# Attention softmax: mask, negation, move to SBUF and row minimum in one VectorE operation

## The chip, the cores and the metric

The kernel runs on one core of a Trainium2 chip. The metric is the device time of one execution, in microseconds (us), median over runs; the profile was taken from one execution on the same core. The engines are TensorE (PE, with its weight loads as PEld), VectorE (DVE), ScalarE (ACT), GpSimd (POOL) and SyncE (SP), which here only issues transfers.

## The reference

A batch of 8 images of 384 channels and 32x32 positions (1024 tokens) goes through two layers, all in float32. Layer 0 is a state-space block: RMS norm, input projection, a short convolution, a scan with 16 states over the tokens forwards and backwards, a gate, an output projection, and a depthwise 3x3 convolution beside it. Layer 1 is attention and a feed-forward network with sign-binarized weights and quantized activations. The change is in the attention:

```python
scores = jnp.einsum('bhqd,bhkd->bhqk', q, k)          # 6 heads of 64
causal = jnp.tril(jnp.ones((T, T), dtype=bool))        # T = 1024
scores = jnp.where(causal, scores, -jnp.inf)
attn = jax.nn.softmax(scores, axis=-1)
out = jnp.einsum('bhqk,bhkd->bhqd', attn, v)
```

The binarization of the two feed-forward weights subtracts the mean of each of five groups of output rows; the change touches how that mean is scaled.

## The kernel before, in words

**The scan** is cut into 768 units of two states by 512 tokens by 128 channels. For each unit POOL multiplies the input by the broadcast B row (`s_first`, L588), ACT makes the decays `da` in PSUM (L601), DVE runs two scans in place in `g` (L606), POOL multiplies by the broadcast C row (L612), and PE adds the unit into the PSUM tile `y` with eight transposing products (`s_sum`, L620). There are six `g` buffers, and POOL's first product for a unit runs two units ahead of the scan (`AHEAD = 2`), so a `g` buffer comes free for POOL when PE has read it at L620.

**The attention** of one image runs over three pairs of heads (`c`) and two halves of the queries (`g`). `probabilities` goes over four blocks of 128 queries (`i`) and, for each, one or two blocks of up to 512 keys (`kb`): 36 pairs of score tiles an image, 288 in all, two heads (`e`) to a pair. For each pair PE makes the scores of the two heads in two PSUM banks (tag `s`, two banks in all; L786), with 64 rows each, and in the blocks that hold the diagonal adds the causal mask by a product of a bf16 identity with a bf16 mask (L797). DVE takes the negated row maximum from PSUM (L808), ACT takes the exponential from PSUM with that as bias, writes it to the SBUF tile `pr` and sums the row (L809). `weighted_values` then transposes the probabilities on PE (L861), ACT copies them to SBUF (L863), PE multiplies them with the values (L874), and DVE scales the product by factors that undo the block maxima (L829 to L838, L888 to L891).

**Order.** The kernel writes its steps into lists with an estimated cost each. `spread_over` merges lists in proportion to their costs: the score steps of one (c, g) are merged with the weighted values of the one before. The scan units are merged with attention and feed-forward steps by due times, so that attention of one image runs beside the scan of the next ones; the attention of the last image of `ORDER` runs alone at the end. The framework's scheduler then fixes the order of each engine's in-order queue; `pin` and `at_once` keep the score products of the two heads next to each other. [...] one bank for `y`, two for `da`, two for `s`, two for `pt`, one for `av`. The SBUF tile `pr` comes from the pool `mid` of ten buffers.

Of the kernel before, what the change touches and what calls it, by code (L numbers as in the profile page):

```python
# [9 lines left out]
F32 = mybir.dt.float32  # L10
BF16 = mybir.dt.bfloat16
AF = mybir.ActivationFunctionType
ALU = mybir.AluOpType
AX = mybir.AxisListType
# [3 lines left out]
P = 128  # L18
B, C, H, W = 8, 384, 32, 32
L = H * W  # L20
NC = C // P
HB = 512
# [9 lines left out]
GROUPS = 5  # L32
# [5 lines left out]
MASKED = -1e30  # L38
# [16 lines left out]
def kernel(  # L55
# [16 lines left out]
    nc = tc.nc  # L72
    pin = tc.keep_in_program_order

    const = ctx.enter_context(tc.tile_pool(name="const", bufs=1))
    small = ctx.enter_context(tc.tile_pool(name="small", bufs=4))
# [7 lines left out]
    def ctile(name, shape, dt=F32):  # L84
        return const.tile(shape, dt, name=name, tag=name)

    def btile(name):
        return big.tile([P, NC, L], F32, name=name, tag="big")

    def mtile(name, n=L):  # L90
        return mid.tile([P, n], F32, name=name, tag="mid")
# [7 lines left out]
    def bank(name, tag=None):  # L99
        if tag is None:  # L100
            turn[0] += 1
            tag = ("s", "pt")[turn[0] % 2]
        return ps.tile([P, HB], F32, name=name, tag=tag, bufs=BANKS[tag])
# [4 lines left out]
    def chunk(c):  # L108
        return slice(c * P, (c + 1) * P)
# [29 lines left out]
    for d in range(2):  # L139
        nc.scalar.dma_start(out=wdt[d * DW : d * DW + RANK, :], in_=w_dt)  # L140
        nc.scalar.dma_start(
            out=wdt[d * DW + RANK : d * DW + RANK + 1, :],
# [12 lines left out]

    ident = ctile("ident", [P, P])
    make_identity(nc, ident)
    identb = ctile("identb", [P, P], BF16)
    nc.vector.tensor_copy(identb, ident)
    cmask = mtile("cmask", P)  # L160
    make_causal_mask(nc, cmask, mask_val=MASKED)
    cmaskb = ctile("cmaskb", [P, P], BF16)
    nc.vector.tensor_copy(cmaskb, cmask)
    onesc = ctile("onesc", [P, P])
    nc.gpsimd.memset(onesc, 1.0 / C)
    onecol = ctile("onecol", [P, 1])
# [29 lines left out]
    def binarize(src, dst, nk, nout, per, name, emit):  # L196

        gs = nout // GROUPS
        st = {}

        def part(w, k, n):
            return w[k * P : (k + n) * P, :].rearrange("(k p) e -> p k e", p=P)

        def view(k, n):
            t = btile(f"{name}_{k}")
            v = t.rearrange("p c l -> p (c l)")[:, : n * nout].rearrange("p (k e) -> p k e", k=n)
            nc.scalar.dma_start(out=v, in_=part(src, k, n))
            return v

        starts = list(range(0, nk, per))  # L210

        @emit
        def _():
            st["ones"] = small.tile([P, P], F32, name=f"ones_{name}", tag="bones", bufs=1)
            nc.vector.memset(st["ones"], 1.0 / (gs * nk * P))
            st["mps"] = bank(f"mps_{name}", "av")

        for k in starts:

            @emit  # L220
            def _(k=k, n=min(per, nk - k)):
                v = view(k, n)
                sums = small.tile([P, GROUPS], F32, name=f"sums_{name}_{k}", tag="bsums", bufs=1)
                for g in range(GROUPS):
                    nc.vector.tensor_reduce(
                        sums[:, g : g + 1], v[:, :, g * gs : (g + 1) * gs], AX.XY, ALU.add
                    )
                nc.tensor.matmul(
                    out=st["mps"][:, :GROUPS],
                    lhsT=st["ones"],  # L230
                    rhs=sums,
                    start=(k == 0),
                    stop=(k == starts[-1]),
                )

        @emit
        def _():
            st["mean"] = small.tile([P, GROUPS], F32, name=f"mean_{name}", tag="bmean", bufs=1)
            nc.vector.tensor_copy(st["mean"], st["mps"][:, :GROUPS])

        for k in starts:

            @emit
            def _(k=k, n=min(per, nk - k)):
                v = view(k, n)
                for g in range(GROUPS):
                    z = v[:, :, g * gs : (g + 1) * gs]
                    nc.vector.tensor_scalar(z, z, st["mean"][:, g : g + 1], None, ALU.subtract)
                t = btile(f"sg_{name}_{k}")
                sg = t.rearrange("p c l -> p (c l)")[:, : n * nout].rearrange("p (k e) -> p k e", k=n)  # L250
                z, sg = v[:, :, : GROUPS * gs], sg[:, :, : GROUPS * gs]
                nc.scalar.activation(sg, z, AF.Sign)
                nc.vector.tensor_tensor(sg, sg, z, ALU.subtract)
                nc.vector.tensor_tensor(z, z, sg, ALU.add)
                nc.vector.memset(v[:, :, GROUPS * gs :], 0.0)
                nc.scalar.dma_start(out=part(dst, k, n), in_=v)
# [417 lines left out]
    def attention(b, emit_ffn, emit):  # L674
        st = {}
# [82 lines left out]
        def at_once(second):  # L758
            return tc.high_priority(offset=HURRY) if second else nullcontext()

        def rows_of(e):
            return slice(e * HD, (e + 1) * HD)

        def blocks_of(n):
            return [(k0, min(k0 + HB, n)) for k0 in range(0, n, HB)]

        def probabilities(c, g, steps):


            nb = g + 1  # L770

            def scores(i, qi, n, kb, k0, k1):
                pr = mtile(f"pr_{b}_{c}_{qi}_{kb}").rearrange("p (e l) -> p e l", e=2)
                st["pr", c, g, i, kb] = pr
                if kb == 0 and i == 0:
                    for what in ("nm", "rs"):
                        st[what, c, g] = small.tile(
                            [P, QT, 2, nb], F32, name=f"{what}_{b}_{c}_{g}", tag=f"{what}{nb}"
                        )
                nm, rs = st["nm", c, g], st["rs", c, g]  # L780
                ss = [bank(f"s_{b}_{c}_{qi}_{kb}_{e}", "s") for e in range(2)]

                order = (1, 0)
                for e in order:
                    with at_once(e == order[1]):
                        mm = nc.tensor.matmul(  # L786
                            out=ss[e][:, : k1 - k0],
                            lhsT=st["q"][rows_of(e), c, chunk(qi)],
                            rhs=st["k"][rows_of(e), c, k0:k1],
                            start=True,  # L790
                            stop=(k1 < n),
                        )
                    if e == order[1]:
                        pin(mm)
                if k1 == n:
                    for e in order:
                        mm = nc.tensor.matmul(  # L797
                            out=ss[e][:, k1 - k0 - P : k1 - k0],
                            lhsT=identb,
                            rhs=cmaskb,  # L800
                            start=False,
                            stop=True,
                        )
                        pin(mm)
                for e in range(2):
                    s = ss[e][:, : k1 - k0]
                    m = nm[:, i, e, kb : kb + 1]
                    nc.vector.tensor_reduce(m, s, AX.X, ALU.max, negate=True)  # L808
                    nc.scalar.activation(  # L809
                        pr[:, e, : k1 - k0], s, AF.Exp, bias=m, accum_out=rs[:, i, e, kb : kb + 1]  # L810
                    )

            for i in range(QT):
                qi = g * QT + i
                n = (qi + 1) * P
                for kb, (k0, k1) in enumerate(blocks_of(n)):
                    steps(lambda i=i, qi=qi, n=n, kb=kb, k0=k0, k1=k1: scores(i, qi, n, kb, k0, k1))
# [404 lines left out]
```

## Time and profile before

| | |
|---|---|
| time, median of 3 runs | 5189.24 us (5177.72 to 5191.12) |
| span of the profiled execution | 5182.2 us, 51037 instructions |
| PE busy | 4203.1 us, 81% |
| PE weight loads busy | 2254.6 us, 44% |
| POOL busy | 3688.1 us, 71% |
| DVE busy | 3562.3 us, 69% |
| ACT busy | 2701.1 us, 52% |
| mean granted TensorE clock | 0.876 of full speed |

A row of the groups gives the line and engine, the operation, what is written from what, the shape, the count, and then the busy time in us with the mean of one in ns, and the idle time of the engine just before these instructions with what ended most of it. A row of waits gives who waited for whom: us in total, times, and the longest. A row of the windows gives the busy time of each engine in one stretch and the number of its instructions. "issue" is time in which the profile shows nothing that was waited for. The busy time of PE is modelled, since its matmuls overlap.

### The profile page before, as it was taken

The numbers are of one execution on the slowest core, as the hardware profiler recorded it, in microseconds if no ns is written. First come the engines' busy times: TensorE is split into PE (matmuls) and PEld (weight loads), VectorE is DVE, ScalarE is ACT, GpSimd is POOL, SyncE is SP. The second block draws the span as 40 slices with busy tenths as digits, with TensorE's granted clock in tenths as the row PEclk, the third lists the DMA queues.
The fourth block names the chain that finished last, engine by engine and source line by source line (L and its number), as shares of the span: only waits on it lengthen the run. The fifth ranks groups of instructions, "written<-read, shape, count | busy, mean of one in ns | idle before, by whom it ended". The sixth has DMA issues, their size and how long they took to land. (4 is left out here: it accounts for less than half of the span.)

```text
span 5182.2 us, 51037 instructions
## 1 busy us (share of the span) xinstructions
PE 4203.1 (81%) x16842; PEld 2254.6 (44%) x16842; DVE 3562.3 (69%) x4206; ACT 2701.1 (52%) x4891; POOL 3688.1 (71%) x1944
## 2 busy tenths in 40 slices
PE   3687787888878788888887888878889888888798
PEld 1243443444434444444543444434445444444444
DVE  6887887667886667876687856778666665565522
ACT  4565564555645556545556445564454454453334
POOL 0578687877679776787777788677878977787600
PEclk7788797889889899898998888988988889989888
DMA  6554545324463234543343533336333234224200
GB/s 228 197 184 152 200 167 190 111 80 156 152 216 114 88 103 146 198 143 112 109 153 121 201 126 103 118 125 221 122 103 126 88 106 166 87 70 150 82 33 25
DMA packets 365009, 696.38 MB, mean 134 GB/s; under 512 B 30104, under 2 KB 88904, under 8 KB 364744
## 3 DMA queue, kind: packets, MB, share of 16 engines
q1 hardware_dynamic: 355232, 676.97, 38.8%
q10 hardware_dynamic: 9512, 16.15, 0.9%
q8 instruction: 133, 2.18, 0.2%
q14 instruction: 132, 1.08, 0.1%
HBM read 527.33 MB, written 165.68 MB: 134 GB/s over the span
## 5 line engine op out<-in xcount | busy, mean ns | idle before, releaser
L588 POOL TENSOR_TENSOR g<-ud,bc 128x1024 f32<-128x1024 f32 x768 | 1836.3, 2391 | 737.0 <-PE y L620 586.5
L612 POOL TENSOR_TENSOR g<-g,bc 128x1024 f32<-128x1024 f32 x768 | 1818.8, 2368 | 229.8 <-DVE g L606 177.2
L601 ACT ACTIVATE da<-dl,amat 128x512 f32<-128x512 f32 x1536 | 1059.6, 692 | 1648.4 <-DVE g L606 1606.5
L606 DVE TENSOR_TENSOR_SCAN g<-da,carry,g 128x512 f32<-128x512 f32 x768 | 955.9, 1271 | 461.6 <-POOL g L588 430.2
L606 DVE TENSOR_TENSOR_SCAN g<-da,g 128x512 f32<-128x512 f32 x768 | 904.2, 1209 | 514.4 <-POOL g L588 496.9
L620 PE MATMUL y<-ident,g 128*128 128x128 f32 x6144 | 948.4, 301 | 272.7 <-POOL g L612 204.3
L620 PEld LDWEIGHTS y<-ident,g 128*128 128x128 f32 x6144 | 787.7, 156 | 663.0 <-POOL g L612 325.3
L786 PE MATMUL s<-k,q 64*128 64x512 f32 (+3 forms) x1152 | 443.6, 616 | 182.3 <-ACT pr L809 172.3
L808 DVE TENSOR_REDUCE nm<-s 128x1 f32<-128x512 f32 (+3 forms) x576 | 293.4, 543 | 231.0 <-PE s L797 154.9
L861 PE MATMUL pt<-ident,pr 128*128 128x128 f32 x1728 | 334.9, 315 | 80.0 <-ACT ptn L863 49.0
L809 ACT ACTIVATE pr<-s,nm 128x512 f32<-128x512 f32 (+3 forms) x576 | 327.8, 573 | 123.5 <-DVE nm L808 122.7
L992 PE MATMUL hp<-t,w 128*128 128x512 f32 x720 | 339.1, 616 | 25.8 <-DMA w<-w1s 15.1
L341 PE MATMUL in<-xn,win 128*128 128x512 f32 x576 | 295.2, 655 | 49.7 <-DVE xc L463 16.6
L1037 PE MATMUL yp<-h,w 128*128 128x512 f32 x720 | 327.5, 612 | 9.0 <-DMA w<-w2s 8.9
L861 PEld LDWEIGHTS pt<-ident,pr 128*128 128x128 f32 x1728 | 221.5, 159 | 238.7 <-ACT ptn L863 118.5
L863 ACT COPY ptn<-pt 128x512 f32<-128x512 f32 (+3 forms) x576 | 264.0, 480 | 101.8 <-PE pt L861 100.1
L874 PE MATMUL av<-ptn,v 128*64 128x512 f32 (+3 forms) x1152 | 287.9, 575 | 35.8 <-DVE o L888 21.0
L786 PEld LDWEIGHTS s<-k,q 64*128 64x128 f32 x1152 | 164.3, 212 | 323.6 <-ACT pr L809 254.8
L725 PE MATMUL qp<-t,wqk 128*128 128x512 f32 x576 | 263.0, 606 | 18.4 <-DVE t L302 13.0
L400 DVE SCALAR_TENSOR_TENSOR loc<-xn,vec,loc 128x496 f32<-128x496 f32 (+3 forms) x384 | 260.4, 721 | 23.6 <-ACT loc L389 22.2
L611 POOL COPY carry<-g 128x2 f32<-128x2 f32 x384 | 83.4, 217 | 248.0 <-DVE g L606 240.3
L1037 PEld LDWEIGHTS yp<-h,w 128*128 128x128 f32 x720 | 139.8, 198 | 176.3 <-issue 165.4
(157 smaller groups left out, 4817.3 us busy)
## 6 DMA issues: line engine op xcount, KB each, us to landing
bc<-rows SPq DMA_DIRECT2D x512, 512.0 KB, 4.1
dl<-sdl SPq DMA_DIRECT2D x160, 256.0 KB, 2.9
ud<-sud SPq DMA_DIRECT2D x160, 256.0 KB, 2.7
t<-st SPq DMA_DIRECT2D x63, 512.0 KB, 5.3
su<-u SPq DMA_DIRECT2D x48, 512.0 KB, 3.7
du<-su SPq DMA_DIRECT2D x96, 256.0 KB, 4.3
sdl<-du SPq DMA_DIRECT2D x96, 256.0 KB, 2.9
sud<-du SPq DMA_DIRECT2D x96, 256.0 KB, 2.7
```

The costliest lines, as they stand in the source:

```text
L341: nc.tensor.matmul(out=mp, lhsT=st["win", c][:, k, i, :], rhs=st["xn"][:, k, half(h)], start=(k == 0), stop=(k == NC - 1),)
L588: pin(nc.gpsimd.tensor_tensor(g, ud, sst["bc", 0, u.b, u.part, u.n], ALU.mult))
L601: nc.scalar.activation(da, sst["dl", u.b, u.c, u.part], AF.Exp, scale=amat[:, u.c, n : n + 1])
L606: nc.vector.tensor_tensor_scan(gi[:, ::step], da[:, ::step], gi[:, ::step], first, ALU.mult, ALU.add)
L612: pin(nc.gpsimd.tensor_tensor(g, g, sst["bc", 1, u.b, u.part, u.n], ALU.mult))
L620: nc.tensor.matmul(out=y[:, j, :], lhsT=g[:, i, chunk(j)], rhs=ident, is_transpose=True, start=(u.opens and i == 0 and j == 0), stop=(u.cl ...
L786: mm = nc.tensor.matmul(out=ss[e][:, : k1 - k0], lhsT=st["q"][rows_of(e), c, chunk(qi)], rhs=st["k"][rows_of(e), c, k0:k1], start=True, st ...
L808: nc.vector.tensor_reduce(m, s, AX.X, ALU.max, negate=True)
L809: nc.scalar.activation(pr[:, e, : k1 - k0], s, AF.Exp, bias=m, accum_out=rs[:, i, e, kb : kb + 1])
L861: nc.tensor.transpose(pt[:, chunk(i)], pr[:, e, chunk(j % QT)], ident)
L992: nc.tensor.matmul(out=hp, lhsT=st["w1"][:, c, chunk(m % 2)], rhs=st["xn"][:, c, half(h)], start=(c == 0), stop=(c == NC - 1),)
L1037: nc.tensor.matmul(out=yp, lhsT=st["w2", k // 6][:, k % 6, :], rhs=st["h", k // NC][:, k % NC, half(h)], start=(k == 0), stop=(k == NF - 1),)
```

## The change

One DVE operation now reads the scores from PSUM and a mask from SBUF, adds them, multiplies by -1, writes the result to `pr`, and gives the row minimum of it, which is the negated row maximum of the masked scores. ACT takes the exponential of `pr` in place, with scale -1 and the minimum as bias. In the blocks that do not hold the diagonal, the mask operand is one zero column, broadcast. The mask products on PE and the bf16 identity go away; the mask is a constant of 512 columns in bf16, zeros ahead of the 128 columns of the triangle. So the two score banks are read by DVE alone, ACT no longer reads them, and the PSUM bank is handed back to PE by the DVE operation. In the binarization the tile of ones is replaced by the constant of 1/384 that is there already, and the copy of the mean scales it.

```diff
-    identb = ctile("identb", [P, P], BF16)
-    nc.vector.tensor_copy(identb, ident)
-    cmask = mtile("cmask", P)
-    make_causal_mask(nc, cmask, mask_val=MASKED)
-    cmaskb = ctile("cmaskb", [P, P], BF16)
-    nc.vector.tensor_copy(cmaskb, cmask)
+    cmask = ctile("cmask", [P, HB], BF16)
+    nc.vector.memset(cmask, 0.0)
+    masked = mtile("masked", P)
+    make_causal_mask(nc, masked, mask_val=MASKED)
+    nc.vector.tensor_copy(cmask[:, HB - P :], masked)
...
-            st["ones"] = small.tile([P, P], F32, name=f"ones_{name}", tag="bones", bufs=1)
-            nc.vector.memset(st["ones"], 1.0 / (gs * nk * P))
...
-                    lhsT=st["ones"],
+                    lhsT=onesc,
...
-            nc.vector.tensor_copy(st["mean"], st["mps"][:, :GROUPS])
+            nc.vector.tensor_scalar(
+                st["mean"], st["mps"][:, :GROUPS], C / (gs * nk * P), None, ALU.mult
+            )
...
-                            stop=(k1 < n),
+                            stop=True,
                         )
                     if e == order[1]:
                         pin(mm)
-                if k1 == n:
-                    for e in order:
-                        mm = nc.tensor.matmul(
-                            out=ss[e][:, k1 - k0 - P : k1 - k0],
-                            lhsT=identb,
-                            rhs=cmaskb,
-                            start=False,
-                            stop=True,
-                        )
-                        pin(mm)
+                w = k1 - k0
+                mask = cmask[:, HB - w :] if k1 == n else cmask[:, :1].to_broadcast([P, w])
                 for e in range(2):
-                    s = ss[e][:, : k1 - k0]
-                    m = nm[:, i, e, kb : kb + 1]
-                    nc.vector.tensor_reduce(m, s, AX.X, ALU.max, negate=True)
+                    x, m = pr[:, e, :w], nm[:, i, e, kb : kb + 1]
+                    nc.vector.tensor_tensor_reduce(
+                        out=x, in0=ss[e][:, :w], in1=mask, scale=-1.0,
+                        scalar=-MASKED, op0=ALU.add, op1=ALU.min, accum_out=m,
+                    )
                     nc.scalar.activation(
-                        pr[:, e, : k1 - k0], s, AF.Exp, bias=m, accum_out=rs[:, i, e, kb : kb + 1]
+                        x, x, AF.Exp, bias=m, scale=-1.0, accum_out=rs[:, i, e, kb : kb + 1]
                     )
```

More of the change, by code (lines that the diff above doesn't have):

```diff
@@ L794, in scores @@
                         pin(mm)
-                if k1 == n:
-                    for e in order:
-                        mm = nc.tensor.matmul(
-                            out=ss[e][:, k1 - k0 - P : k1 - k0],
-                            lhsT=identb,
-                            rhs=cmaskb,
-                            start=False,
-                            stop=True,
-                        )
-                        pin(mm)
-                for e in range(2):
-                    s = ss[e][:, : k1 - k0]
-                    m = nm[:, i, e, kb : kb + 1]
-                    nc.vector.tensor_reduce(m, s, AX.X, ALU.max, negate=True)
+                w = k1 - k0
+                mask = cmask[:, HB - w :] if k1 == n else cmask[:, :1].to_broadcast([P, w])
+                for e in range(2):
+                    x, m = pr[:, e, :w], nm[:, i, e, kb : kb + 1]
+                    nc.vector.tensor_tensor_reduce(
+                        out=x,
+                        in0=ss[e][:, :w],
+                        in1=mask,
+                        scale=-1.0,
+                        scalar=-MASKED,
+                        op0=ALU.add,
+                        op1=ALU.min,
+                        accum_out=m,
+                    )
                     nc.scalar.activation(
-                        pr[:, e, : k1 - k0], s, AF.Exp, bias=m, accum_out=rs[:, i, e, kb : kb + 1]
+                        x, x, AF.Exp, bias=m, scale=-1.0, accum_out=rs[:, i, e, kb : kb + 1]
                     )
```

## Prediction

> **What bounds the kernel now.** I read the groups first, for what the touched lines cost; then the waits, for what they hold up; then the windows, for the stretches in which they run; then the timeline of the last attention, which has no scan beside it. The groups (page):
>
> ```profile
> L588 POOL TENSOR_TENSOR g<-ud,bc 128x1024 f32<-128x1024 f32 x768 | 1836.3, 2391 | 737.0 <-PE y L620 586.5
> L612 POOL TENSOR_TENSOR g<-g,bc 128x1024 f32<-128x1024 f32 x768 | 1818.8, 2368 | 229.8 <-DVE g L606 177.2
> ...
> L786 PE MATMUL s<-k,q 64*128 64x512 f32 (+3 forms) x1152 | 443.6, 616 | 182.3 <-ACT pr L809 172.3
> L808 DVE TENSOR_REDUCE nm<-s 128x1 f32<-128x512 f32 (+3 forms) x576 | 293.4, 543 | 231.0 <-PE s L797 154.9
> ...
> L809 ACT ACTIVATE pr<-s,nm 128x512 f32<-128x512 f32 (+3 forms) x576 | 327.8, 573 | 123.5 <-DVE nm L808 122.7
> ```
>
> POOL needs 2.39 + 2.37 = 4.76 us a unit, 3655 us for 768, and is idle before its first product mainly until PE has emptied a `g` buffer. PE stands before the scores until ACT has read the score bank, DVE stands before the maximum mostly until a mask product is done. The waits (whole run) say the same from the waiting side:
>
> ```profile
> POOL g L588 <- PE y L620: 586.5, 211, 11.3
> PEld s L786 <- ACT pr L809: 254.8, 273, 6.3
> ...
> PE s L786 <- ACT pr L809: 172.3, 141, 6.0
> ...
> DVE nm L808 <- PE s L797: 154.9, 55, 44.4
> ...
> ACT pr L809 <- DVE nm L808: 122.7, 99, 3.8
> ```
>
> So there is a ring: ACT holds the score bank, PE waits in its in-order queue, the transposes of `y` queued behind the scores come late, and POOL waits for them. By the starts of L808 the score steps fill seven stretches beside the scan (199, 211, 209, 208, 215, 204 and 196 us, 1442 us in all) and 146 us alone at the end. The windows of the first and the last of them (columns: stretch, length, PE, PEld, DVE, ACT, POOL busy, clock):
>
> ```profile
> 931.00:1130.00 199.00, 162.82 (x879) 92.85 (x877) 135.23 (x172) 116.62 (x281) 170.62 (x87) 0.87 0.29 100
> ...
> 4999.00:5145.00 146.00, 129.29 (x584) 58.84 (x583) 43.99 (x95) 70.63 (x206) 0.00 (x0) 0.80 0.01 4
> ```
>
> In the first, POOL (171 of 199) and PE (163) are close to full, DVE has 64 us free and ACT 82. The waits of each of the seven stretches give POOL for PE at L620 24.5, 37.3, 37.5, 26.1, 33.8, 33.4, 42.5, in sum 235 us, and PE for ACT at L786 157 us; POOL for any work of DVE under 16 us. So beside the scan PE's delay binds POOL, and DVE does not. At the end the chain is scores, mask, maximum, exponential, next scores (timeline: start, us, engine):
>
> ```profile
> 5005.94 2.63 PE L786 MATMUL s<-k,q 64*128 64x512 f32 x4 [0.82 <-ACT pr L809]
> ...
> 5008.50 0.40 PE L797 MATMUL s<-cmaskb,identb 128*128 128x128 bf16 x2
> ...
> 5008.83 1.29 DVE L808 TENSOR_REDUCE nm<-s 128x1 f32<-128x512 f32 x2 [3.18 <-PE s L797]
> 5009.56 0.69 ACT L809 ACTIVATE pr<-s,nm 128x512 f32<-128x512 f32 x1 [3.11 <-DVE nm L808]
> ...
> 5010.38 0.50 PEld L786 LDWEIGHTS s<-k,q 64*128 64x128 f32 x2 [1.46 <-ACT pr L809]
> ```
>
> The next scores begin 0.13 us after the first exponential, though DVE was done with that bank about 0.85 us earlier.
>
> [...] The new operation has one input in PSUM and one in SBUF. [...]
>
> ```profile
> L528 DVE TENSOR_TENSOR du<-du 128x512 f32<-128x512 f32 x96 | 117.3, 1228 | 0.2
> ...
> L703 DVE SCALAR_TENSOR_TENSOR t<-op,rssm,t 128x512 f32<-128x512 f32 x48 | 34.4, 734 | 21.2 <-PE op L695 21.1
> ...
> L606 DVE TENSOR_TENSOR_SCAN g<-da,g 128x512 f32<-128x512 f32 x768 | 904.2, 1209 | 514.4 <-POOL g L588 496.9
> ```
>
> [...] an operation that also writes its accumulator is two instructions. DVE has none in this trace; the build of the changed kernel shows the second one, and ACT's form of it is in the trace at 197 ns. [...]
>
> **The change part by part.**
>
> *PE, bank release.* Each of 121 waits beside the scan (157 us, 1.3 us each) now ends with DVE's operation. One exponential (327.8 / 576 = 0.57 us) and its place behind `da` exponentials (0.69 us each, taken as 0.3 on average) drop out, and 0.15 us for the accumulator read is added. That is 0.7 us, and 0.95 in the two pairs of three that hold the diagonal, where a mask product also stood in the chain (below): on average 0.87 x 121 = 105 us of PE time. The wait that remains is on DVE. Behind the waiting scores are PE's transposes of `y`, for which POOL waits, as before.
>
> *PE, mask products.* 384 go. They show 61.9 us busy, but the weight load after a pair starts 0.09 us after the pair does (5008.50 to 5008.59), so a pair really takes between 0.09 and 0.3 us of PE: 168 pairs beside the scan give 15 to 50, I take 21 us. For DVE the scores are ready some 0.25 us sooner.
>
> *From PE time to time.* 105 + 21 = 126 us of PE in the seven stretches. POOL can use it only where it waits for PE (235 us of its 263 idle), and not every shortened stall is followed by a POOL wait. I take 65%: -82 us.
>
> *DVE.* The main operation: between the maximum (676 ns at 512) and L703's 734, taken as 700: 576 x 0.02 = 12 us. The read: lower bound ACT's pace (two exponentials of 384 start 0.57 us apart, as long as one, so the read hides but for 0.1), upper bound ACT's 0.197: 0.1 x 576 = 58 us. The broadcast column: 192 operations of 512, [...] I take 0.1, 19 us. Sum 89 us, seven eighths of it beside the scan: 78. DVE is free there for 32% of the time and POOL rarely waits for it, but the scans stand behind the operation in DVE's queue; a quarter shows: +19 us. `pr` must now be free when DVE starts, not when ACT does; no row shows ACT waiting for it, and the built order shows the same ten buffers in the same turn, so nothing.
>
> *ACT.* The exponential reads SBUF: L523, SBUF to SBUF with a bias, is 715 against 680 at 512, so 20 us on ACT in all, hidden in its 48% idle time.
>
> *The last attention.* PE's 15 us of stall end almost wholly (-13), 24 mask pairs leave the chain (0.25 us each, half of it seen: -3), some pairs of scores run closer together because both banks are free (-4), and DVE's read adds about 0.1 x 36 = +4. Sum -16.
>
> *Order.* In the built queues DVE's score operations stand a few places earlier among the scans (up to 7), and 822 of 12360 common PE instructions move by more than ten places: either sign, 0, and up to 30 us into the range. The constants and the binarization: a few operations under 0.2 us, nothing.
>
> Sum: -82 + 19 - 16 = -79, and another -10 for weight loads that now start before a stall ends (254.8 us of such waits, mostly the same time): 5189 - 89 = 5100.
>
> **The rivals.**
>
> *More than that.* PE's pairs of scores take 1.13 to 2.63 us for the same four products in the last attention, the short ones where both banks were free. With earlier release most are short and POOL's 235 us shrink by two thirds (-157); with the end 5030. For it: PE and POOL are both near full. Against: DVE waits for POOL's first product 50 to 60 us a stretch anyway.
>
> *Only the end gains.* The stalls of PE move from ACT to DVE, whose operation stands behind two scans of 1.2 us, and the extra 78 us on DVE delay POOL's second product: beside the scan nothing, at the end -16: about 5170. For it: L612 waits 177 us for DVE over the run. Against: under 16 us of POOL's waits for DVE fall into the stretches.
>
> *Slower.* The operation carries a running minimum, and the one row here that carries a value from column to column, the scan, takes 1209 against 676 at 512. At that pace and the mean of 384 columns it costs 0.4 us more, and with the read 0.55 x 72 = 40 us a stretch: DVE goes from 135 to 175 of 199 and becomes the bound together with POOL. A stretch then grows by some 6 us, the end by 36 x 0.25 = 9: 5240. Against: the maximum of L808 is carried too, at 676.
>
> **How the numbers follow.** 5100 at 0.50; 5030 at 0.20; 5170 at 0.17 (of which 0.07 lies within 0.3%, above 5173.7); 5240 at 0.13. Faster 0.80, same 0.07, slower 0.13. The range from 5020 to 5200 holds the first three with their unknowns and leaves out most of the last.
>
> **What would show it.** L797 gone; the operation at 0.65 to 0.75 us for 512 columns with a mask, and the broadcast form apart; waits of PE at L786 named DVE, about 40 to 60 us in place of 172; POOL's wait at L588 for PE near 500 in place of 586; the seven stretches at about 190 us, the last near 130. Wrong if the operation takes over 1 us, if POOL's waits for DVE grow by as much as those for PE shrink, or if the stretches keep their length.

## The result, and the profile after

The changed kernel takes 5047.77 us, median of 4 runs (5044.19 to 5052.02), against 5187.74 us before in the same comparison. The ratio is 0.9734, 95% interval 0.9717 to 0.9751: 140 us or 2.7% faster. Forecast were 5100 us and a range from 5020 to 5200.

The groups of the changed kernel (page; line, engine, operation, count, then busy us, mean ns, idle us before and what ended it). The lines have moved: the DVE operation is L800, the exponential L810, the transposes of the probabilities L862, the copies of them L864.

```profile
L588 POOL TENSOR_TENSOR g<-ud,bc 128x1024 f32<-128x1024 f32 x768 | 1839.3, 2395 | 652.0 <-PE y L620 513.1
L612 POOL TENSOR_TENSOR g<-g,bc 128x1024 f32<-128x1024 f32 x768 | 1820.5, 2371 | 228.4 <-DVE g L606 175.6
...
L786 PE MATMUL s<-k,q 64*128 64x512 f32 (+3 forms) x1152 | 405.1, 610 | 122.9 <-DVE nm L800 111.5
L800 DVE CUSTOM_DVE_ANT_0 pr<-s,cmask 128x512 f32<-128x512 f32 (+3 forms) x576 | 300.6, 545 | 212.6 <-PE s L786 185.8
L810 ACT ACTIVATE pr<-pr,nm 128x512 f32<-128x512 f32 (+3 forms) x576 | 348.8, 606 | 141.7 <-DVE nm L800 139.5
```

The mask products are gone, POOL's own work is what it was, and POOL waits 513 us for PE in place of 586. The same groups with shapes kept apart, for the price of the operation and of the read of its minimum:

```profile
L800 DVE CUSTOM_DVE_ANT_0 pr<-s,cmask 128x512 f32<-128x512 f32 x288 | 190.0, 677 | 90.5 <-PE s L786 90.3
...
L800 DVE DVE_READ_ACCUMULATOR2_ANT nm<- 128x1 f32 x576 | 47.4, 82 | 0.0
```

677 ns at 512 columns: the same as the plain maximum before (676). The mean of the 288 holds masked and unmasked tiles, and the longest of all 576 is 694 ns, so the broadcast column costs nothing extra. The waits (who waited for whom; us, times, longest):

```profile
POOL g L588 <- PE y L620: 513.1, 211, 10.7
...
DVE pr L800 <- PE s L786: 185.8, 104, 43.6
POOL g L612 <- DVE g L606: 175.6, 20, 18.8
...
PE s L786 <- DVE nm L800: 111.5, 105, 4.0
...
DVE pr L800 <- PE pt L862: 26.2, 10, 5.7
```

PE's wait at the scores has changed its name from ACT to DVE and fell by 61 us only. POOL's wait for DVE did not grow. The last row is new: `pr` must be free when DVE starts, and ten times it was not. The windows of the first score stretch and of the last attention (stretch, length, then PE, PEld, DVE, ACT, POOL busy, clock):

```profile
926.00:1116.00 190.00, 153.66 (x820) 87.11 (x821) 136.08 (x243) 118.84 (x283) 168.19 (x84) 0.86 0.30 103
4915.00:5014.00 99.00, 93.55 (x537) 45.61 (x538) 45.52 (x167) 72.45 (x207) 0.00 (x0) 1.00 0.00 1
```

From the start of its first to the start of its last score operation on DVE (the measure of all tables below), the seven stretches beside the scan take 188, 192, 206, 192, 192, 208 and 185 us, in sum 1364 against 1445 before: -81. The last attention takes 98 against 146 us: -48, and its granted clock is 1.00 where it was 0.80, so its PE work shows 94 us busy in place of 129. The remaining 4 us of the 133 between the two profiled spans lie outside these eight stretches.

The timeline of the last attention of the changed kernel (start, us, engine) shows the short ring:

```profile
4920.05 0.69 DVE L800 CUSTOM_DVE_ANT_0 pr<-s,cmask 128x512 f32<-128x512 f32 x1 [0.74 <-PE s L786]
4920.67 0.08 DVE L800 DVE_READ_ACCUMULATOR2_ANT nm<- 128x1 f32 x1
...
4920.79 0.72 ACT L810 ACTIVATE pr<-pr,nm 128x512 f32<-128x512 f32 x1 [0.61 <-DVE nm L800]
4920.81 0.29 PEld L786 LDWEIGHTS s<-k,q 64*128 64x128 f32 x2 [1.14 <-DVE nm L800]
4920.81 1.73 PE L786 MATMUL s<-k,q 64*128 64x512 f32 x4 [0.31 <-DVE nm L800]
```

The read ends at 4920.75, and both the exponential and the next scores start within 0.06 us of that, side by side. Before, the scores began only after the exponential.

### The profile page after: what moved, and what is told of

Read it like the earlier page. It is cut to its first block, busy times and chain, and to the rows that moved or that the text cites. A ratio compares the mean times of both kernels' runs of the same rounds, so it can differ in the third digit from the quotient of the medians.

```text
span 5049.4 us, 50760 instructions
## 1 busy us (share of the span) xinstructions
PE 4101.8 (81%) x16458; PEld 2191.0 (43%) x16458; DVE 3599.9 (71%) x4780; ACT 2721.4 (54%) x4891; POOL 3691.4 (73%) x1944
## 5 line engine op out<-in xcount | busy, mean ns | idle before, releaser
L620 PE MATMUL y<-ident,g 128*128 128x128 f32 x6144 | 932.4, 299 | 270.7 <-POOL g L612 214.6
L620 PEld LDWEIGHTS y<-ident,g 128*128 128x128 f32 x6144 | 772.5, 154 | 729.1 <-POOL g L612 339.9
L786 PE MATMUL s<-k,q 64*128 64x512 f32 (+3 forms) x1152 | 405.1, 610 | 122.9 <-DVE nm L800 111.5
L800 DVE CUSTOM_DVE_ANT_0 pr<-s,cmask 128x512 f32<-128x512 f32 (+3 forms) x576 | 300.6, 545 | 212.6 <-PE s L786 185.8
L810 ACT ACTIVATE pr<-pr,nm 128x512 f32<-128x512 f32 (+3 forms) x576 | 348.8, 606 | 141.7 <-DVE nm L800 139.5
L862 PE MATMUL pt<-ident,pr 128*128 128x128 f32 x1728 | 301.9, 305 | 73.5 <-ACT ptn L864 32.9
L862 PEld LDWEIGHTS pt<-ident,pr 128*128 128x128 f32 x1728 | 209.1, 153 | 237.2 <-ACT ptn L864 88.6
L875 PE MATMUL av<-ptn,v 128*64 128x512 f32 (+3 forms) x1152 | 276.6, 563 | 23.9 <-DVE o L889 16.2
L864 ACT COPY ptn<-pt 128x512 f32<-128x512 f32 (+3 forms) x576 | 255.2, 474 | 74.0 <-PE pt L862 72.6
L786 PEld LDWEIGHTS s<-k,q 64*128 64x128 f32 x1152 | 138.4, 208 | 251.8 <-DVE nm L800 187.6
```

What stands on the lines that cost most here:

```text
L620: nc.tensor.matmul(out=y[:, j, :], lhsT=g[:, i, chunk(j)], rhs=ident, is_transpose=True, start=(u.opens and i == 0 and j == 0), stop=(u.cl ...
L786: mm = nc.tensor.matmul(out=ss[e][:, : k1 - k0], lhsT=st["q"][rows_of(e), c, chunk(qi)], rhs=st["k"][rows_of(e), c, k0:k1], start=True, st ...
L810: nc.scalar.activation(x, x, AF.Exp, bias=m, scale=-1.0, accum_out=rs[:, i, e, kb : kb + 1])
L862: nc.tensor.transpose(pt[:, chunk(i)], pr[:, e, chunk(j % QT)], ident)
L875: mm = nc.tensor.matmul(out=av[rows_of(e), cols], lhsT=st["v"][:, j, hd * HD : (hd + 1) * HD], rhs=st["ptn", j, e][:, cols], start=(j % QT ...
```

## The experiments

My theory was that of the prediction: the bank comes back an exponential earlier, the mask products go, PE has more time, and POOL waits less. The first rival was that one of the two parts does it alone; a second one appeared on the way: that the queue order, which the framework's scheduler makes anew for each kernel, does it. All ratios are against the kernel before on the same chip; the first row of the tables is the run beside the changed kernel.

### One part at a time

The first kernel is the one before without the mask products, the second the changed one with the mask back on PE, the third the changed one with the exponential reading PSUM again, so that ACT holds the bank.

```diff
# e1_no_mask, from the kernel before
-                if k1 == n:
-                    for e in order:
-                        mm = nc.tensor.matmul(... lhsT=identb, rhs=cmaskb, start=False, stop=True)
# e2_mask_on_pe, from the changed kernel
+                if k1 == n:
+                    for e in order:
+                        mm = nc.tensor.matmul(... lhsT=identb, rhs=cmaskb, start=False, stop=True)
-                mask = cmask[:, HB - w :] if k1 == n else cmask[:, :1].to_broadcast([P, w])
+                mask = cmask[:, :1].to_broadcast([P, w])
# e3_hold_bank, from the changed kernel (every tile with the zero column, no causal mask)
-                        x, x, AF.Exp, bias=m, scale=-1.0, accum_out=...
+                        x, ss[e][:, :w], AF.Exp, bias=m, accum_out=...
```

> The kernel before without the mask products on PE, nothing in their place (the causal mask is left out of the result); the bank is still held until ACT's exponential. If the earlier release of the bank is the cause (my theory), little comes: 20 to 40 us less than before, ratio 0.992 to 0.996, the last attention still near 135 to 145 us and PE still waiting about 150 us for ACT at the scores. If the mask products are the cause (rival), most of the 140 us comes: ratio 0.980 or less, the last attention near 105 us.

> The changed kernel with the mask products put back on PE and the broadcast zero column as the mask operand of every DVE operation; the result is the same. Early-release theory: 100 to 120 us less than before, ratio 0.977 to 0.981. Mask rival: 20 to 60 us less, ratio 0.988 or more. The broadcast operand in all 576 operations also shows whether it costs: 512 columns at 677 ns as before if not[...].

> The changed kernel (no mask products, same DVE operation with its write) but ACT takes the exponential from the PSUM bank again, so the bank is held until ACT is done; the zero column is the mask operand everywhere, so the causal mask is left out of the result. Early-release theory: most of the gain is gone, ratio 0.990 to 1.005, PE waits at the scores name ACT again with about 150 us. Mask rival: ratio 0.980 or less.

| kernel | time, us | ratio, 95% | seven stretches, us | last, us (clock) |
|---|---|---|---|---|
| before | 5187.74 | 1 | 1445 | 146 (0.80) |
| e1_no_mask | 5129.83 | 0.9894 (0.9861 to 0.9928) | 1400 | 143 (0.76) |
| e2_mask_on_pe | 5087.05 | 0.9814 (0.9797 to 0.9830) | 1385 | 106 (1.00) |
| e3_hold_bank | 5137.79 | 0.9909 (0.9895 to 0.9924) | 1412 | 130 (0.88) |
| changed | 5047.77 | 0.9734 (0.9717 to 0.9751) | 1364 | 98 (1.00) |

Groups by shape of e2_mask_on_pe, in which every tile has the broadcast column as its mask operand:

```profile
L814 DVE CUSTOM_DVE_ANT_0 pr<-s,cmask 128x512 f32<-128x512 f32 x288 | 188.0, 679 | 57.9 <-PE s L789 47.1 <-PE s L801 10.5
```

679 ns: the broadcast column is as cheap as the mask itself. Put together, the masks are worth 58 us (before to e1) or 39 us (e2 to changed), the release 101 us (before to e2) or 90 us (e3 to changed), and the DVE operation with its read costs 8 us (e1 to e3, less than the spread of e1's four times, 5114 to 5148). That looks like a clean sum of the prediction's own terms, with the masks two to three times as large. It is not clean, because each of these kernels also has its own queue order. In the built queues (counted over the 576 score tiles) a score product of e1 has on average 3.3 transposes of `y` fewer ahead of it than before, of e3 3.3, of e2 4.8, and of the changed kernel 5.1. A score operation of DVE stands 1.1, 1.1, 1.1 and 1.6 scan operations earlier. So these three runs give the price of a part together with the order that the part brings.

By its ratio e1 lies between its two forecasts, e2 just short of the range of the early release (0.977 to 0.981), and e3 within it. The forecast of the waits failed: in e1 and e3, where ACT holds the bank as before, PE was to wait about 150 us for ACT at the scores. PE's waits at the scores in e1, e2 and e3, in this order:

```profile
PE s L786 <- ACT pr L799: 99.5, 101, 4.1
...
PE s L789 <- DVE nm L814: 150.4, 126, 4.4
...
PE s L786 <- ACT pr L810: 106.7, 118, 4.1
```

With the bank held, e1 and e3 stall no longer than the changed kernel (111 us), and e2, which stalls longest, is the fastest of the three. So this stall does not tell which kernel is fast. POOL's wait for PE before its first product goes with the times: 567, 524 and 573 us.

### What a microsecond of DVE costs, and a surprise

To price DVE's time, the operation was issued twice.

```diff
# e6_twice_dve, from the changed kernel
-                    nc.vector.tensor_tensor_reduce(...)
+                    for _ in range(2):
+                        nc.vector.tensor_tensor_reduce(...)
```

> The changed kernel with the DVE operation issued twice on the same data, so each score tile costs DVE twice (348 us of DVE more over the run) and the bank comes free that much later. If DVE's time beside the scan is hidden but for a quarter, as the prediction took it, plus the chain of the last attention: 80 to 130 us more than the changed kernel, ratio 0.99 to 1.00. If DVE is at its limit once the operation is dear (the rival that ends slower): ratio 1.01 or more. If DVE's time is fully hidden: below 0.98.

It took 5005.5 us (4996 to 5011.8), ratio 0.9652 (0.9636 to 0.9667): 42 us faster than the changed kernel, with 234 us more of DVE busy. Its waits:

```profile
POOL g L588 <- PE y L620: 278.6, 109, 10.8
POOL g L612 <- DVE g L606: 225.3, 44, 18.8
...
PE s L786 <- DVE nm L801: 51.1, 69, 4.0
```

POOL's wait for PE is nearly halved, and its wait for DVE grew by 50 us. The stretches shrink from 1364 to 1253 us, while the last attention, without a scan beside it, grows from 98 to 136 and the time between the stretches by 27. The ratio lies below the 0.98 of "fully hidden", but that the kernel would beat the changed one was in no forecast. In one and the same order the second operation lengthens the stretches, from 1164 to 1253 us (e7 and e6, below), so it is not what shortens them here, and the order was compared: in the built queues DVE's score operations stand 4.4 scan operations earlier than before (1.6 in the changed kernel), while PE's scores are back behind as many transposes of `y` as before (+0.3). The start of the first stretch in PE's queue (Y: transposes of `y`, S: score products, a: weighted values; mask products of before left out):

```
before    Y8 S2 Y8 S2 Y10 S2 Y6 a4 Y6 S2 a2 Y2 S2 a2 Y7 S1 Y2 a3 Y2 S1 Y1 a8 S2 a9 S1 a1 S1 ...
changed   Y8 S2 Y8 S2 Y5 S2 Y3 S2 Y1 S1 Y4 S1 Y3 a8 S2 Y8 a8 S2 Y8 S2 a12 Y4 a2 Y4 S3 ...
twice     Y8 S2 Y8 S2 Y10 S2 Y6 a4 Y1 S2 a2 Y7 S2 a2 Y5 a3 Y1 a3 S1 a2 S1 Y2 a5 S2 a9 Y4 S1 ...
```

### The order held fixed

To part order and operations, the program is traced twice: once in another form, only to take its queue order, and once in the form that runs, with issue-order edges (no waits) along those queues. The core of it:

```diff
+    def program(new, order=None):
+        ...
+            traced = [i for i in nc.cur_bb.bb.instructions if i.name not in EXTRA]
+            for queue in order or ():
+                for k, n in zip(queue, queue[1:]):
+                    tc.add_manual_dep(traced[n], traced[k].name, <NoSync>)
...
+    nc = program(<the form that runs>, program(<the form that gives the order>)[1])[0]
```

`EXTRA` are instructions that only one form has, such as the mask products and the second DVE operation. Three kernels were made so: the changed operations in the order of the twice form (e7), the changed operations in an order near that of the kernel before (e8; DVE's score operations left free among the others, 0.3 scans earlier on average), and the operations of before in the order of the changed kernel (e9).

The traces show how far this worked. In e7 and e9 the queues of PE, DVE, ACT and POOL follow the order that was asked for, instruction by instruction. In e8 they do not quite, because the form that gives its order has the operations of before but the constants of the changed kernel, and the scheduler ordered it a little differently: 1315 of PE's 16458 products stand elsewhere than in the kernel before, 411 of them by more than ten places, where the changed kernel has 4304 and 1266. A score product of e8 has as many transposes of `y` ahead of it as before (+0.05 on average), a transpose of the probabilities 0.8 more.

> The changed kernel with one VectorE operation a score tile, but with the queues of PE, DVE, ACT and POOL in the order that the scheduler chose when that operation stood there twice (the kernel that took 5005.5 us). If the order alone made that kernel faster, this one keeps its gain beside the scan (104 us) and gets back the 39 us that the second operation cost in the last attention: 4900 to 4975 us, POOL's wait at L588 for PE under 300 us. If the gain came from the longer time that DVE needed (scores released later, so fewer collisions), this one is back at 5048 us +- 15, POOL's wait for PE near 513. In between, if both count.

> The changed kernel, operation for operation, with the queues of PE, ACT and POOL in the order that the scheduler chose for the kernel before (its mask products taken out of the row), DVE's score operations left free among the others in their old order. In that order 5.1 more transposing products of y on average stand ahead of a score product than in the changed kernel's own. The prediction put the order at 0: then this takes 5048 us +- 15. If the changed kernel lost time by scores moved ahead of y, this is faster: 4960 to 5020 us, POOL's wait at L588 for PE 350 to 450 us in place of 513. If the changed kernel's own order was part of its gain, it is slower: 5065 to 5110 us.

> The operations of the kernel before (mask products, maximum and exponential from PSUM), with the queues of PE, DVE, ACT and POOL in the order that the scheduler chose for the changed kernel, each operation in the place of the one that answers to it. If the order brings the gain and the operations nothing beside the scan, the seven stretches take about 1376 us as in the changed kernel and only the last attention stays long (146 in place of 99 us): about 5095 us. If the order pays only where the score bank comes back early (scores are moved ahead of y, and a held bank then stops PE with y behind it), the stretches are as long as before or longer: 5180 to 5230 us. If the effects of order and operations simply add, with the last attention counted in, about 5045 us.

| operations | order of | time, us | ratio, 95% | seven stretches, us | last, us (clock) |
|---|---|---|---|---|---|
| before | before | 5187.74 | 1 | 1445 | 146 (0.80) |
| changed | near before (e8) | 5193.81 | 1.0005 (0.9995 to 1.0016) | 1480 | 113 (0.98) |
| before | changed (e9) | 5180.98 | 0.9981 (0.9972 to 0.9990) | 1433 | 154 (0.73) |
| changed | changed | 5047.77 | 0.9734 (0.9717 to 0.9751) | 1364 | 98 (1.00) |
| changed | twice (e7) | 4903.35 | 0.9448 (0.9427 to 0.9469) | 1164 | 113 (1.00) |

The middle of the table is the finding. In an order near the old one the operations bring nothing, which no forecast of e8 allowed for; the new order without the operations brings 0.2%; the two together bring 2.7%. Two of these steps are clean: from e9 to the changed kernel the order is the same and the operations are worth 133 us, and from the changed kernel to e7 the operations are the same and the order is worth 144 us. The waits of e8:

```profile
POOL g L599 <- PE y L631: 635.1, 208, 11.5
...
PE s L797 <- DVE nm L832: 86.6, 79, 2.8
```

PE's stall at the scores is half of that before (87 against 172 us), yet POOL waits 635 us for PE, more than before the change. Summed over the seven stretches, PE waits 123 us before the transposes of the probabilities, for the copies and exponentials of ACT (89 and 34); before the change it waited 41 us there for the copies and never for the exponentials, in the changed kernel 23 and never. So about as much as was won at the scores (157 to 84 us in the stretches) was lost a few places further on in the same queue. Of the 123 us, 107 fall on transposes that stand at the same place as before; whether the places that did move play a part is not shown. The waits of e9, the old operations in the new order (L810 is its mask product):

```profile
POOL g L600 <- PE y L632: 588.9, 232, 9.5
...
DVE nm L823 <- PE s L810: 305.8, 131, 44.4
ACT pr L824 <- DVE nm L823: 298.8, 189, 4.9
...
PE s L798 <- ACT pr L824: 148.6, 164, 3.6
```

The time lies at the lower edge of the second forecast (5180 to 5230 us), and POOL's wait for PE is where it was before the change (589 against 587 us). The reason given in that forecast, that scores moved ahead of `y` meet a held bank and stop PE, is not shown: PE's stall at the scores is below that of before (149 against 172 us), while DVE's wait for the mask products has doubled (306 against 155 us). Nor do e1 and e3 fit it. They hold the bank too, and have the scores 3.3 transposes of `y` earlier, yet their stretches are 45 and 33 us shorter than before, where e9 gains 12. What they lack is the mask products. So it may be those, and not the held bank, that keep the new order from paying in e9; a kernel with the bank held, no mask products and exactly the new order would tell, and was not run. The waits of e7, the fastest kernel here:

```profile
PE y L627 <- POOL g L619: 328.3, 157, 14.3
...
POOL g L595 <- PE y L627: 285.5, 110, 10.0
...
POOL g L619 <- DVE g L613: 191.2, 31, 18.8
...
PE s L793 <- DVE nm L808: 10.1, 16, 2.4
```

and its window of the first stretch:

```profile
925.00:1088.00 163.00, 137.62 (x828) 79.46 (x828) 125.61 (x235) 113.34 (x274) 156.19 (x76) 0.95 0.32 107
```

The time is in the first forecast, that of the order alone. PE's stall at the scores is 10 us over the whole run. Now PE waits for POOL more than POOL for PE, and over the seven stretches (windows of 1175 us in whole) POOL is busy 1105 us, 94%. POOL's 286 us of waiting for PE lie outside the stretches; in them less than 1 us of it is left, beside 47 us for DVE. Against the changed kernel the stretches give 200 us, the last attention takes 15 back, and the time between them 34: a shorter stretch holds less of the scan (467 of POOL's products in place of 498), so more of it is left for the other parts. PE's granted clock over the stretches is 0.92 in place of 0.86, and nearly the same number of PE products in them (5963 and 5956) takes 1008 us in place of 1116. Whether this clock is part of the cause beside the scan or goes along with a fuller PE was not tested. From e6 to e7 the order stays and the second operation goes: 5005.5 to 4903.4 us, so 576 operations with their reads, 262 us of DVE busy, cost 102 us.

### The clock in the last attention

Is the clock in the last attention a cause, or does it only go along? The kernel before got ten spare bf16 products per pair of score tiles in the last attention, into a PSUM bank that is free there.

```diff
# e5_warm, from the kernel before
+                if b == ORDER[-1]:
+                    spare = bank(f"spare_{b}_{c}_{qi}_{kb}", "y")
+                    for _ in range(10):
+                        mm = nc.tensor.matmul(out=spare[:, :P], lhsT=identb, rhs=cmaskb, start=True, stop=True)
+                        pin(mm)
```

> The kernel before, with ten spare bf16 products of 128 columns behind every pair of scores in the last attention, written to a PSUM bank that nothing reads: PE gets about 20 us more work there and no wait is removed. If PE's granted clock (0.80 there) falls because of its gaps, and the slow clock is itself a good part of the stretch: clock over 0.9 and the last attention shorter, 115 to 140 us in place of 146, ratio 0.994 to 0.999. If the clock is not a matter of the gaps: the last attention gets 10 to 20 us longer, ratio 1.002 to 1.004.

It took 5169.83 us, ratio 0.9972 (0.9962 to 0.9982), within its first forecast. Windows of 12 us inside the last attention, first of the kernel before:

```profile
4999.00:5011.00 12.00, 8.47 (x27) 4.00 (x26) 3.56 (x8) 4.50 (x16) 0.00 (x0) 0.65 0.00 0
...
5083.00:5095.00 12.00, 10.57 (x24) 3.76 (x25) 3.00 (x5) 3.97 (x12) 0.00 (x0) 0.57 0.00 0
5107.00:5119.00 12.00, 11.63 (x76) 5.79 (x75) 4.29 (x7) 6.38 (x17) 0.00 (x0) 1.00 0.00 1
```

and of the kernel with the spare products 132 us of the last attention, with the row of its spare products:

```profile
5001.00:5133.00 132.00, 124.24 (x932) 69.57 (x930) 45.49 (x100) 71.09 (x208) 0.00 (x0) 1.00 0.02 5
```

```profile
L808 PE MATMUL spare<-cmaskb,identb 128*128 128x128 bf16 x360 | 26.4, 219 | 0.0
```

Before, the clock swings between 0.57 and 1.00 within the attention; with the gaps filled it stays at 1.00. Though PE has 26 us more to do, the stretch is 15 us shorter (146 to 131); its other work shows 124.2 - 26.4 = 98 us busy in place of 129. So the clock is a cause of its own: with the time of the spare products taken off, it gives 15 of the 48 us that the changed kernel gains there. (The scheduler also moved 36 products of this attention by more than ten places, and the share of that was not measured.) The low clock of before, with window means down to 0.57, took no long pause: the longest gap in PE's modelled busy time there is 1.1 us. By what rule the clock follows PE's work the runs do not show. Whether the score banks alone, with a second pair of them in the last attention, would close the gaps was not measured.

## Why the prediction was right, and where it was wrong

The direction and the range were right, and the size beside the scan was close: -73 forecast for the stretches (-82, +19, -10), -81 measured. That closeness is luck, because the way to the number was not right.

**The step that failed is "Order".** It read that the built order moves score operations a few places, "either sign, 0, and up to 30 us into the range". In an order near that of before, the changed operations take 5194 us: the new order is worth about 146 us to the changed operations and 0.2%, some 10 us, to the old ones. I had the shift of the queues in hand and took it for noise. In its place the runs show that the new order and the new operations pay only together: in the new order exactly, the operations are worth 133 us. Which of the operations the order needs, the early release or the end of the mask products, the runs do not part.

**PE, bank release** (105 us of PE time, 65% of it shown). In the order near the old one, the whole change gave +35 us beside the scan and -33 in the last attention. The stall fell as foreseen in kind, but its 65% did not reach POOL: about as much time came back as waits at the transposes of the probabilities. The forecast of 40 to 60 us for the wait that remains at L786 was wrong too: it is 111, and 87 and 10 in the orders of e8 and e7, so the wait hangs on the order.

**PE, mask products** (21 us). Taking them away was worth 58 and 39 us, but with an order of its own each time; what the products alone cost stays open.

**DVE** (+89 us busy, +19 shown). The operation at 677 ns against 700 taken, the read 82 ns against 100, the broadcast nothing against 19 us in sum, which was my estimate with no row behind it: DVE's busy time grew by 38 us only (3562.3 to 3599.9). That the operation would run like L703 and not like L528, with both sources in SBUF, was my estimate too: L528 has a mean of 1228 ns but a median of 682 and a longest of 2834, and what stretches it was not shown. The share of a quarter was low: from e6 to e7 102 of 262 us show, 39%, a part of it in the last attention. That `pr` must be free when DVE starts was put at nothing; DVE waits 26 us for it, and what this costs is not shown.

**ACT** (+20 us, hidden). 2701.1 to 2721.4 us, exactly that; the exponential from SBUF takes 713 ns at 512 columns where the one from PSUM took 680.

**The last attention** (-16, measured -48). The mechanism was right, the size was off, and a missing term is the granted clock: as the gaps closed it went from 0.80 to 1.00. PE's busy time fell by 36 us to 94 of 99, of which the mask products are 8 and the rest goes with the clock. The operations carry this: 146 to 113 us near the old order, where PE's queue in this attention is the old one but for 16 products, and 154 to 98 in the new one; the clock goes with them in both (0.80 to 0.98 and 0.73 to 1.00).

**The rivals.** "Only the end gains" is closest to what the operations do near the old order, though there the loss beside the scan eats the gain at the end. "Slower" fell with the 677 ns. "More than that" asked for POOL's wait to shrink by two thirds; it took another order to reach that. Two readings of the prediction were a little off, without weight: from first to last start its seven stretches come to 1445 us, not 1442, and POOL's waits for DVE in them to 17 us, not under 16.

Three things stay open. How the early release and the end of the mask products each reach POOL is one, as said above. What exactly in the twice form's order pays is not shown: it differs from the changed one both in PE's queue, where `y` comes first again, and in DVE's, where the score operations come before some three more scans. And why the scheduler moves the scores was not tested: e1, which only drops the mask products, already has 3.3 of the 5.1 places, so the early release cannot be the only reason.

## What to carry to other kernels

When a scheduler sets the queues, an edit changes the order of everything around it, so an experiment that takes one part away prices the part and its order together; hold the order fixed before you give a part its number, and compare the queues in the traces afterwards, since the order you get may not quite be the one you asked for. Where two engines wait for each other through queues, look at the order before the cost of the operations: here it was worth 290 us between two orders of the same operations, more than twice the change itself. In a stretch where PE waits again and again, read the granted clock next to the waits: here ten spare products per pair of score tiles took the clock from 0.80 to 1.00 and the stretch from 146 to 131 us. And a longer stall in front of an instruction need not mean a slower kernel: among e1, e2 and e3 the one that stalls most at the scores (150 us against 100 and 107) is the fastest (5087 us against 5130 and 5138).

## What the runs showed of the hardware that was not expected

- A DVE operation with a PSUM source, an SBUF mask, an SBUF result and a running minimum takes 677 ns at 512 columns, no more than the plain maximum from PSUM (676); as mask operand a bf16 column read again for all columns costs the same as a full bf16 mask (679 ns with nothing else).
- The read of its minimum is a second instruction of 82 ns on DVE, where ACT's read of its sum takes 188 ns in the same kernel (197 before).
- Ten spare products per pair of score tiles, 26 us of PE in all, made a stretch 15 us shorter, while the granted clock went from 0.80 to 1.00.
